# A graph layer on one core: Sel's transfers on another queue, sign counts spread over tiles, products in larger groups, and the residual added after the loop

## The chip, the cores and the metric

The kernel runs on one core of one Trainium2 chip. The metric is the device time of one execution in microseconds (us), lower is better. The core has five engines with a queue of instructions each: PE (TensorE, matrix products), DVE (VectorE), ACT (ScalarE), POOL (GpSimd) and SP (SyncE, which here only issues DMAs). DMAs can be issued from SP, ACT and POOL. Each queue is worked in order, so an instruction that waits holds up all that is behind it.

## The reference

The graph has 6,250 nodes with 128 channels, and 206,250 edges sorted by their destination (100,000 random pairs in both directions, and a loop at each node). W is 128 x 256, b has 128 elements.

```python
h = maximum(layernorm(x), 0)
feat = concatenate([h[dst], h[src] - h[dst]], axis=-1)
msg = feat @ W.T + b
out = segment_max(msg, dst, num_segments=6250)
return x + where(isfinite(out), out, 0)
```

A message splits into a part of the destination and a part of the source: with A = h (W1 - W2)^T + b and B = h W2^T, where W1 and W2 are the halves of W, the message of an edge is A[dst] + B[src]. A[dst] is the same for all edges of a node, so the output is x + A + the maximum of B over the node's sources.

## The kernel before

**Layout.** The nodes are cut two ways. By destination: partition p of 128 holds 49 nodes (LD = 49), and loads from the edge lists a window of 1,792 edges (WIN) that begins at its first one. By source: 6,250 = 50 x 125, a source is row q (0 to 49) and place l (0 to 124). A one-hot product over l can fetch B of one source for each node from the table Bp, which holds B in SBUF. What this dense path can't take, the repeated hits of a node in one row q, is left to a stream of up to 512 residual edges per partition (NS = REST = 512), gathered from DRAM.

**Prologue (0 to 191 us of the profile).**
- x is loaded in seven groups of eight rows q (`load_x`, line 290), 0 to 2 on SP and ACT, 3 to 6 on SP behind a small DVE memset each. `moments` (lines 360, 362) and `scales` (368, 372, 373) give the mean and the deviation.
- `step` makes two rows q of A and B: normalise and transpose (`norm`, `turn`, 549, 554), `relu` (558), `weigh` (564, 566), `keep_all` (ACT's copy to a tile `ba`, 571), `piece` and `less` (574, 578). There are two `ba` tiles, each of two steps, so a copy into one waits for the landing of the `store` from it (586), which SP issues. 27 calls of `step` are written into the program by hand: six ahead of the tests, the others between other work.
- DVE finds the windows: the number of blocks below (343), a gather of one block (98), a count in it (401), then gathers of dwin (destinations) and swin (sources). Lines 616 to 624 make the keys.
- 46 tests, each a DVE comparison of the keys with themselves shifted (493; 501 and 507 for the last three), which PE adds up into `dup` by an identity matrix (488), find repeated pairs. The last two tests compare with the bounds LOb and HIb. There are three tiles `eq` between DVE and PE.
- Eleven moves and `spread` pack the residual edges: `ridx` their sources, `sdl` their destinations.
- POOL writes constants meanwhile: Sel (440), LOb and HIb (458, 459, 28 memsets), and others. Sel, the selector of a row q, goes through DRAM (SelD): it is written, patched in four places and read back (466 to 472), on SP.

**Main loop (191 to 905 us).** 13 tiles of ten partitions' nodes (490 columns; the last tile has 392), each 25 pairs of rows i, i+1: 325 pairs, numbered k. In a pair:
- `some(mats, ...)`: PE makes a few of the 140 small products (246) of the next tile's V, whose factors are the one-hot tiles OHQ (ACT's signs, 203) and OHD (DVE, 208). Once all are done, four steps follow, one a pair: copy out (251), `diff` (255), `rows_u` (258), `rows_t` (261, 262). They end in Vf, which holds for each node and row q the place l.
- `z_and_onehot` of the next pair: PE's z (738), ACT's oh (739).
- PE's four products ps with Bp (786), and DVE's maximum with acc2 (788 for the first pair of a tile, then 790).
- the stream: `gather_group` issues eight gathers of B rows from DRAM on POOL (98) into one of six tiles G; `stream_step` takes one row per partition (163), a running maximum within a node, and SP stores each finished group to M (167). `RATE` says how many rows are due after pair k: int(1.65 (k + 1)).
- ACT's signs and DVE's values for the tile after the next.

Two things stand beside this. In tile 1, `sign(c)` counts for each of 49 + 1 limits how many residual edges are below it (748, 50 in all, two a pair); at the start of tile 3 DVE makes from these the row of M that holds each node's result (`last_e`). In the last tile, A is loaded to `xa` (770), x in four pieces to `xo` (807), and DVE adds them (812) between the pairs.

**End (905 to 951 us).** When the stream is through, POOL issues 49 gathers from M (`extract`, 98). For each group of eight, PE transposes the accumulator, DVE takes the maximum with the gathered rows (850), adds xa (855), and SP and ACT store the output (862).

The counts that the change touches most stand in these lines:

```python
def sign(c):
    dump = two.tile([P, NS], BF16, name="dump", bufs=1)
    A_.activation(dump, sdl, AF.Sign, scale=2.0, bias=nbias[:, c:c + 1], accum_out=ends[:, c:c + 1])
...
while state["ran"] < min(NS, int((k + 1) * RATE)):
    if state["gathered"] < NG and state["ran"] >= (state["gathered"] - GB + 1) * U:
        gather_group()
    stream_step()
```

Of the kernel before, what the change touches and what calls it, by code (L numbers as in the profile page):

```python
# [29 lines left out]
F32 = mybir.dt.float32  # L30
BF16 = mybir.dt.bfloat16
# [9 lines left out]
P = 128  # L41
# [6 lines left out]
L = 125  # L48
LD = 49
# [3 lines left out]
U = 8  # L53
# [9 lines left out]
def gnn_kernel(tc, x, src, dst, W, b, out):  # L63
    nc = tc.nc
# [36 lines left out]
    with ExitStack() as ctx:  # L101
# [10 lines left out]
        with ExitStack() as body:  # L112
# [154 lines left out]
            with ExitStack() as pre:  # L267
# [79 lines left out]
                blk = swin[:, :SB]  # L347
                gather(blk, dst.rearrange("(b s) -> b s", s=SB), below_i[:, 0:1])

                kk = pool.tile([P, REST], F32, name="kk")  # L350
# [59 lines left out]

                for g in (3, 4, 5, 6):
                    xg[g] = rows.tile([P, U, C], F32, name="G") if g < 6 else pool.tile([P, Q % U, C], F32, name="xt")
                    V.memset(xg[g][:L, 0, 0:1], 0.0)
                    load_x(g, (nc.sync, nc.sync))

                for i in range(2):
# [20 lines left out]

                LOb = work.tile([P, W2], BF16, name="LOb", bufs=1)
                HIb = work.tile([P, W2], BF16, name="HIb", bufs=1)
                G_.memset(Sel.rearrange("p q m -> p (q m)").bitcast(F32), 0.0)  # L440
# [13 lines left out]
                for j, f in enumerate((100.0, -100.0)):  # L454
                    G_.affine_select(out=adj[:, j:j + 1], in_=adj[:, j:j + 1], compare_op=ALU.not_equal, fill=f,
                                     base=1 - P, pattern=[[0, 1]], channel_multiplier=1)
                for b in range(NBLK):
                    G_.memset(LOb[:, b * P:(b + 1) * P], float(lo[b] + 1))
                    G_.memset(HIb[:, b * P:(b + 1) * P], float(hi[b] + 1))
                G_.iota(nbias, pattern=[[-2, LD + 1]], base=-1, channel_multiplier=0,  # L460
# [4 lines left out]

                nc.sync.dma_start(SelD, Sel)
                for i, k in enumerate((0, 64)):
                    nc.sync.dma_start(at(SelD, k * Q * (L + 1), [[(Q + 1) * (L + 1), Q], [1, L + 1]]), dg[:, i])
                for q in range(2):
                    nc.sync.dma_start(SelD[Q + q:Q + q + 1], cm[Q + q:Q + q + 1].rearrange("p (o m) -> p o m", o=1)  # L470
                                      .to_broadcast([1, Q, L + 1]))
                nc.sync.dma_start(Sel, SelD)

# [140 lines left out]
                for _ in range(6):  # L614
                    step()
                V.tensor_scalar(dlf, dwin, thr, 1.0, op0=ALU.subtract, op1=ALU.add)
                V.tensor_scalar(dlc, dlf, 0.0, float(LD + 1), op0=ALU.max, op1=ALU.min)
# [12 lines left out]
                for n, f in enumerate(tests):  # L630
                    f()
                    if n % 8 == 5:
                        step()
                    elif n % 5 == 2 and early:
                        turned(*early.pop(0))
                    if n in (16, 32):
                        moments(3 + n // 32)
                        scales_a(3 + n // 32)
                    if n in (18, 34):
                        scales_b(3 + n // 32)  # L640
# [79 lines left out]
            with ExitStack() as main:  # L720
# [21 lines left out]
                def some(fs, left):  # L742
                    for f in fs[:-(-len(fs) // max(left, 1))]:
                        fs.pop(0)()

                def sign(c):
                    dump = two.tile([P, NS], BF16, name="dump", bufs=1)
                    A_.activation(dump, sdl, AF.Sign, scale=2.0, bias=nbias[:, c:c + 1], accum_out=ends[:, c:c + 1])  # L748

                oh = z_and_onehot(*pairs[0])  # L750
                soon, hot_fs = list(onehots(1)), [[], []]
                mats, rest = [], []
                RATE = 1.65
                XG = 13
# [3 lines left out]
                for k, (t, i) in enumerate(pairs):  # L758
# [18 lines left out]

                    if t or not (soon[0] or soon[1]):
                        some(mats, left - 4)
                    nxt = z_and_onehot(*pairs[k + 1]) if k + 1 < len(pairs) else None  # L780
# [8 lines left out]
                    else:  # L789
                        V.tensor_tensor(acc2[:, :, :n], acc2[:, :, :n], ps[:, :, :n], ALU.max)  # L790
                    while state["ran"] < min(NS, int((k + 1) * RATE)):
                        if state["gathered"] < NG and state["ran"] >= (state["gathered"] - GB + 1) * U:
                            gather_group()
                        stream_step()
                    if state["ran"] == NS and not Rt:
                        for d in range(LD):
                            extract(d)
                    if xa is not None and i >= 16 and (i - 16) % 8 == 0 and (i - 16) // 8 * XG < LD:

                        d0 = (i - 16) // 8 * XG  # L800
                        d1 = min(d0 + XG, LD)
                        xo = fin.tile([P, XG, C], F32, name="xo", bufs=2)
                        if d1 > LASTD:
                            V.memset(xo[96:], 0.0)
                        for p0, p1, g in ((0, P - 16, d1), (P - 16, P - 1, d1), (P - 1, P, min(d1, LASTD))):
                            if g > d0:
                                nc.sync.dma_start(xo[p0:p1, :g - d0],
                                                  at(x, (p0 * LD + d0) * C, [[LD * C, p1 - p0], [1, (g - d0) * C]]))
                        adds.append((d0, d1, xo))
                    if adds and (i - 16) % 8 == 6:  # L810
                        d0, d1, xo = adds.pop(0)
                        V.tensor_add(xa[:, d0:d1], xa[:, d0:d1], xo[:, :d1 - d0])  # L812
                    for fs in soon:
                        some(fs, 10 - i // 2)
                    for fs in hot_fs:
                        some(fs, left)
                    oh = nxt
                    if i == Q - 2:
# [3 lines left out]
                                          for j in range(2)), ALU.max)  # L822
                    if t == 1:
                        sign(i)
                        sign(i + 1)
                    if t == 3 and i == 0:

                        V.tensor_scalar(ends, ends, -0.5, 0.5 * NS, op0=ALU.mult, op1=ALU.add)
                        V.tensor_tensor(has, ends[:, 1:], ends[:, :LD], ALU.is_gt)
                        V.tensor_scalar(ends, ends, -1.0, 0.0, op0=ALU.add, op1=ALU.max)  # L830
                        V.tensor_scalar(ends, ends, rowbase, float(-P * NS), op0=ALU.add, op1=ALU.add)
                        V.tensor_tensor(has, has, ends[:, 1:], ALU.mult)
                        V.tensor_scalar_add(last_e, has, float(P * NS))
# [6 lines left out]
                T_.matmul(p[:1, 0, :16], ones[:, :1], badc, start=True, stop=True)  # L840
                acc_v = acc.rearrange("c (p d) -> c d p", d=LD)
                for d0 in range(0, LD, U):
                    g = min(U, LD - d0)
                    o = fin.tile([P, U, C], F32, name="o", bufs=2)
                    for j0 in range(0, g, 4):
# [79 lines left out]
```

## Time and profile before

| | us |
|---|---|
| median of three runs | 954.12 |
| lowest and highest | 952.63, 956.5 |
| the profiled execution | 952.84 |
| its span | 951.0 |
| PE busy | 773.3 (81%) |
| DVE busy | 763.7 (80%) |
| ACT busy | 654.1 (69%) |
| POOL busy | 561.1 (59%) |

The span runs from the first to the last instruction of the program in one profiled execution; its own device time is 1.84 us longer. A busy time is the union of an engine's instructions. Times in timelines count from the start of the span, L12 is line 12 of the kernel, and what stands in brackets behind an instruction is how long its engine was idle before it and what ended that. PEld is PE's loading of weights. PEclk is the share of full clock that PE was granted. A tile's name on the left of an arrow is what is written, on the right what is read.

### The profile page before, as it was taken

The page shows a single profiled execution, that of the slowest core. Times are in us where ns is not written, and L with a number is a line of the kernel's source. Part 1 is how long each engine was busy: PE and PEld are TensorE (multiplying, and loading weights), DVE is VectorE, ACT ScalarE, POOL GpSimd, SP SyncE. Part 2 cuts the span into 40 slices and gives each one's busy share as a digit, 9 for nine tenths or more (in the row PEclk, how much of TensorE's full clock was granted, in tenths as well). Part 3 has the DMA queues.
Part 4 walks back from the last instruction along what each step waited for, and adds up shares of the span by engine and source line. Part 5 has one row for each costly group of instructions (what it writes and reads, how often), then busy time and mean ns, then how long its engine had stood idle before and what let it go on. Part 6 is the DMA issues. An engine that isn't in the chain of part 4 may idle for free.

```text
span 951.0 us, 14067 instructions
## 1 busy us (share of the span) xinstructions
PE 773.3 (81%) x4277; PEld 535.0 (56%) x4277; DVE 763.7 (80%) x1799; ACT 654.1 (69%) x1623; POOL 561.1 (59%) x632
## 2 busy tenths in 40 slices
PE   1949658879887789898989898999989898976540
PEld 0424335446555467676767676676767676755430
DVE  5739999785766669897989899798979899996742
ACT  1403484796799988887888888798978887554200
POOL 3300000077777767777777777777777777731774
PEclk9969955685778779997999899899979999998865
DMA  5531011223223223333333333333333333337442
GB/s 139 155 105 44 22 42 46 76 73 97 90 81 97 76 92 119 96 105 111 95 98 119 95 121 97 96 119 97 118 96 109 109 100 114 114 105 229 111 135 82
DMA packets 50518, 95.73 MB, mean 101 GB/s; under 512 B 12209, under 2 KB 31318, under 8 KB 50081
## 3 DMA queue, kind: packets, MB, share of 16 engines
q1 hardware_dynamic: 31108, 55.39, 17.3%
q0 software_dynamic: 18320, 38.92, 15.7%
q10 hardware_dynamic: 1009, 0.49, 0.3%
q8 instruction: 34, 0.56, 0.2%
q14 instruction: 47, 0.39, 0.1%
HBM read 50.05 MB, written 44.64 MB: 100 GB/s over the span
## 4 chain that ended last, share of the span: by engine, by line
PE 57%; ACT 20%; POOL 6%; DVE 6%; DMA 6%; issue 4%; SPq 1%; POOLq 0%; ACTq 0%; DVEq 0%
PE ps L786 25%; PE z L738 16%; PE pv L246 10%; ACT oh L739 7%; ACT OHQ L203 5%; POOL G L98 4%; ACT dump L748 4%; PE pm L564 2%; DVE eq L493 1%; DMA At<-ba 1%; DMA xo<-in_x 1%; DMA SelD<-Sel 1%; PE pv L255 1%; PE dup L488 1%; ACT Vf L262 1%
## 5 line engine op out<-in xcount | busy, mean ns | idle before, releaser
L98 POOL DMA_INDIRECT G<-Bt,ridx x512 | 492.7, 962 | 236.9 <-issue 135.2
L786 PE MATMUL ps<-oh,Bp 126*128 126x490 f32 (+1 forms) x1300 | 435.6, 462 | 20.2 <-DVE acc L790 16.1
L790 DVE TENSOR_TENSOR acc<-acc,ps 128x980 f32<-128x980 f32 (+1 forms) x312 | 360.8, 1157 | 84.7 <-PE ps L786 83.5
L739 ACT ACTIVATE oh<-z 126x490 fp32r<-126x490 f32 (+1 forms) x650 | 336.1, 570 | 134.8 <-PE z L738 134.2
L786 PEld LDWEIGHTS ps<-oh,Bp 126*128 126x128 f32 x1300 | 272.0, 211 | 102.0 <-DVE acc L790 23.8
L738 PE MATMUL z<-Vf,Sel 114*126 114x490 f16 (+1 forms) x650 | 222.0, 421 | 43.9 <-ACT Vf L262 26.8
L203 ACT ACTIVATE OHQ<-TQ,sbias 128x140 bf16<-128x140 bf16 (+1 forms) x637 | 221.3, 408 | 0.6
L163 DVE SCALAR_TENSOR_TENSOR G<-G,slim 128x128 f32<-128x128 f32 x511 | 179.1, 350 | 9.1 <-DMA G<-Bt,ridx 2.0
L246 PEld LDWEIGHTS <-OHQ 128*51 128x51 bf16 x1792 | 108.4, 180 | 101.8 <-issue 91.1
L246 PE MATMUL pv<-OHD,OHQ 128*51 128x13 bf16 (+5 forms) x1638 | 123.4, 244 | 7.7 <-ACT OHQ L203 7.7
L738 PEld LDWEIGHTS <-Sel 114*126 114x126 f16 x650 | 74.0, 146 | 43.2 <-issue 30.5
L208 DVE SCALAR_TENSOR_TENSOR OHD<-TD,TV 128x30 bf16<-128x30 bf16 (+5 forms) x637 | 87.8, 185 | 0.0
L98 POOL DMA_INDIRECT G<-M,last_e x48 | 50.6, 1053 | 46.7 <-DVE xa L812 32.3
L564 PE MATMUL pm<-wT,hT 128*125 128x256 f32 x100 | 48.0, 580 | 20.6 <-ACT hT L558 20.6
L200 POOL MEMSET OHQ<- 128x140 bf16 x4 | 0.8, 227 | 80.8 <-DMA At<-ba 80.8
L488 PE MATMUL dup<-eq,identb 128*128 128x512 bf16 (+1 forms) x184 | 41.5, 366 | 5.0 <-DVE eq L493 2.4
L564 PEld LDWEIGHTS pm<-wT,hT 128*125 128x125 f32 x100 | 22.8, 278 | 28.0 <-ACT hT L558 27.0
L493 DVE TENSOR_TENSOR eq<-KA 128x1792 bf16<-128x1792 int16 x21 | 22.8, 1085 | 18.8 <-PE dup L488 18.8
L748 ACT ACTIVATE dump<-sdl,nbias 128x512 bf16<-128x512 f32 x50 | 35.9, 718 | 0.8
L574 ACT CAST Bp<-pm 125x256 fp32r<-125x256 f32 x50 | 18.5, 370 | 21.0 <-PE pm L578 20.1
L488 PEld LDWEIGHTS <-identb 128*128 128x128 bf16 x184 | 18.4, 101 | 24.1 <-issue 9.5
L788 DVE COPY acc<-ps 128x980 f32<-128x980 f32 (+1 forms) x13 | 15.1, 1163 | 14.9 <-PE ps L786 14.7
(196 smaller groups left out, 420.9 us busy)
## 6 DMA issues: line engine op xcount, KB each, us to landing
M<-G SPq DMA_DIRECT2D x64, 512.0 KB
G<-Bt,ridx POOLq DMA_INDIRECT x512
xa<-At SPq DMA_DIRECT2D x1, 2744.0 KB
G<-in_x SPq DMA_DIRECT2D x6, 448.0 KB
Bt<-ba SPq DMA_DIRECT2D x12, 224.0 KB
At<-ba SPq DMA_DIRECT2D x12, 224.0 KB
xo<-in_x SPq DMA_DIRECT2D x3, 728.0 KB
out_x<-o SPq DMA_DIRECT2D x3, 512.0 KB
```

Source lines behind the costliest of these rows:

```text
L98: G_.indirect_dma_start(out=o, out_offset=None, in_=table, in_offset=bass.IndirectOffsetOnAxis(ap=idx, axis=0))
L163: V.scalar_tensor_tensor(G[:, j], state["prev"], slim[:, k:k + 1], G[:, j], op0=ALU.min, op1=ALU.max)
L203: A_.activation(oq[:, a, :, :nl], TQ[:, :, ls], AF.Sign, scale=2.0, bias=sbias[:, a:a + 1])
L208: V.scalar_tensor_tensor(o[:, bs_, :nl], TD[:, bs_, ls], float(d + 1), TV[:, bs_, ls], op0=ALU.is_equal, op1=ALU.mult)
L246: T_.matmul(o, oq[:, :, b_, l], r, start=k == 0 and b_ == 0, stop=b_ == NBLK - 1, skip_group_check=True)
L488: T_.matmul(dup[:, c0:c1], identb, e[:, c0:c1], start=s == 1, stop=s == SH + 3)
L564: T_.matmul(pm[:L, j], st["hT", i][:, j, :L], wT, start=j == 0, stop=False, skip_group_check=True)
L738: T_.matmul(z[:, :n], Sel[:, i + j], Vf[t % 2][:, :n], start=True, stop=True)
L739: A_.activation(oh[:, j, :n], z[:, :n], AF.Relu)
L748: A_.activation(dump, sdl, AF.Sign, scale=2.0, bias=nbias[:, c:c + 1], accum_out=ends[:, c:c + 1])
L786: T_.matmul(ps[:, j, :n], Bp[:, e, i + j], oh[:, j, :n], start=e == 0, stop=e == 1)
L790: V.tensor_tensor(acc2[:, :, :n], acc2[:, :, :n], ps[:, :, :n], ALU.max)
```

## The change

- Sel's six DMAs are issued on POOL's queue instead of SP's.
- x's groups 4, 5 and 6 are loaded later: 4 after the six steps that precede the tests, 5 and 6 after tests 4 and 8. Their DVE memsets go.
- The 28 memsets of LOb and HIb stand right after the gather of the block.
- `sign(c)` runs once every four pairs, from pair 48 to pair 244 (so one in tile 1, and 49 in tiles 2 to 9); `last_e` is made at pair 248.
- V's products are made in every second pair only, twice as many each time (14, then 13; the last six in pair 20).
- The signs of OHQ are spread over the first 20 pairs of a tile instead of 25.
- The stream is due at 2.05 rows a pair in tile 0 and 1.6 after it.
- xo's first two pieces are loaded in pairs 8 and 16 of the last tile and added after the loop, the other two loaded and added after it.

```diff
                 gather(blk, dst.rearrange("(b s) -> b s", s=SB), below_i[:, 0:1])
+                LOb = work.tile([P, W2], BF16, name="LOb", bufs=1)
+                HIb = work.tile([P, W2], BF16, name="HIb", bufs=1)
+                for b in range(NBLK):
+                    G_.memset(LOb[:, b * P:(b + 1) * P], float(lo[b] + 1))
+                    G_.memset(HIb[:, b * P:(b + 1) * P], float(hi[b] + 1))
...
-                for g in (3, 4, 5, 6):
-                    xg[g] = rows.tile([P, U, C], F32, name="G") if g < 6 else pool.tile([P, Q % U, C], F32, name="xt")
-                    V.memset(xg[g][:L, 0, 0:1], 0.0)
-                    load_x(g, (nc.sync, nc.sync))
+                xg[3] = rows.tile([P, U, C], F32, name="G")
+                V.memset(xg[3][:L, 0, 0:1], 0.0)
+                load_x(3, (nc.sync, nc.sync))
...
-                for b in range(NBLK):
-                    G_.memset(LOb[:, b * P:(b + 1) * P], float(lo[b] + 1))
-                    G_.memset(HIb[:, b * P:(b + 1) * P], float(hi[b] + 1))
...
-                nc.sync.dma_start(SelD, Sel)
+                G_.dma_start(SelD, Sel)
                 for i, k in enumerate((0, 64)):
-                    nc.sync.dma_start(at(SelD, k * Q * (L + 1), [[(Q + 1) * (L + 1), Q], [1, L + 1]]), dg[:, i])
+                    G_.dma_start(at(SelD, k * Q * (L + 1), [[(Q + 1) * (L + 1), Q], [1, L + 1]]), dg[:, i])
                 for q in range(2):
-                    nc.sync.dma_start(SelD[Q + q:Q + q + 1], cm[Q + q:Q + q + 1].rearrange("p (o m) -> p o m", o=1)
+                    G_.dma_start(SelD[Q + q:Q + q + 1], cm[Q + q:Q + q + 1].rearrange("p (o m) -> p o m", o=1)
                                       .to_broadcast([1, Q, L + 1]))
-                nc.sync.dma_start(Sel, SelD)
+                G_.dma_start(Sel, SelD)
...
                 for _ in range(6):
                     step()
+                load_x(4, (nc.sync, nc.sync))
...
                     f()
+                    if n in (4, 8):
+                        load_x(5 + n // 8, (nc.sync, nc.sync))
...
+                def load_xo():
+                    d0 = (adds[-1][1] if adds else 0)
+                    d1 = min(d0 + XG, LD)
+                    xo = fin.tile([P, XG, C], F32, name="xo", bufs=2)
+                    if d1 > LASTD:
+                        V.memset(xo[96:], 0.0)
+                    for p0, p1, g in ((0, P - 16, d1), (P - 16, P - 1, d1), (P - 1, P, min(d1, LASTD))):
+                        if g > d0:
+                            nc.sync.dma_start(xo[p0:p1, :g - d0],
+                                              at(x, (p0 * LD + d0) * C, [[LD * C, p1 - p0], [1, (g - d0) * C]]))
+                    adds.append((d0, d1, xo))
+
+                def add_xo(n):
+                    d0, d1, xo = adds[n]
+                    V.tensor_add(xa[:, d0:d1], xa[:, d0:d1], xo[:, :d1 - d0])
...
-                RATE = 1.65
+                def due(k):
+                    return min(NS, int(2.05 * min(k, NP_) + 1.6 * max(k - NP_, 0)))
...
-                    if t or not (soon[0] or soon[1]):
-                        some(mats, left - 4)
+                    if (t or not (soon[0] or soon[1])) and i // 2 % 2 == 0:
+                        some(mats, (left - 4) / 2)
...
-                    while state["ran"] < min(NS, int((k + 1) * RATE)):
+                    while state["ran"] < due(k + 1):
...
-                    if xa is not None and i >= 16 and (i - 16) % 8 == 0 and (i - 16) // 8 * XG < LD:
...
-                    if adds and (i - 16) % 8 == 6:
-                        d0, d1, xo = adds.pop(0)
-                        V.tensor_add(xa[:, d0:d1], xa[:, d0:d1], xo[:, :d1 - d0])
+                    if xa is not None and i in (16, 32):
+                        load_xo()
...
-                    for fs in hot_fs:
-                        some(fs, left)
+                    for fs, late in zip(hot_fs, (5, 0)):
+                        some(fs, left - late)
...
-                    if t == 1:
-                        sign(i)
-                        sign(i + 1)
-                    if t == 3 and i == 0:
+                    if k % 4 == 0 and 0 <= k // 4 - NP_ // 2 <= LD:
+                        sign(k // 4 - NP_ // 2)
+                    if k // 4 - NP_ // 2 == LD + 1 and k % 4 == 0:
...
+                for n in range(2):
+                    add_xo(n)
+                    load_xo()
                 for d0 in range(0, LD, U):
                     g = min(U, LD - d0)
+                    if d0 + g > adds[1][1] >= d0:
+                        add_xo(2)
+                        add_xo(3)
```

More of the change, by code (lines that the diff above doesn't have):

```diff
@@ L435, in gnn_kernel @@
                     scales_b(g)
-                LOb = work.tile([P, W2], BF16, name="LOb", bufs=1)
-                HIb = work.tile([P, W2], BF16, name="HIb", bufs=1)
                 G_.memset(Sel.rearrange("p q m -> p (q m)").bitcast(F32), 0.0)
@@ L742, in some @@
                 def some(fs, left):
-                    for f in fs[:-(-len(fs) // max(left, 1))]:
+                    for f in fs[:math.ceil(len(fs) / max(left, 1))]:
                         fs.pop(0)()
@@ L797, in gnn_kernel @@
                             extract(d)
-                    if xa is not None and i >= 16 and (i - 16) % 8 == 0 and (i - 16) // 8 * XG < LD:
[L800 to L809, printed above, removed]
-                    if adds and (i - 16) % 8 == 6:
-                        d0, d1, xo = adds.pop(0)
-                        V.tensor_add(xa[:, d0:d1], xa[:, d0:d1], xo[:, :d1 - d0])
+                    if xa is not None and i in (16, 32):
+                        load_xo()
                     for fs in soon:
                         some(fs, 10 - i // 2)
-                    for fs in hot_fs:
-                        some(fs, left)
+                    for fs, late in zip(hot_fs, (5, 0)):
+                        some(fs, left - late)
                     oh = nxt
```

## The prediction

> **What bounds the kernel now.** I read the busy time by tile first. A tile is one of the 13 rounds of the main loop (25 pairs of rows i, i+1), cut at the DVE copy of line 788 that opens each. One tile and the two ends stand out.
>
> ```profile
> core 0: us, PE busy (x) PEld busy (x) DVE busy (x) ACT busy (x) POOL busy (x), PEclk, DMA share, GB/s
> 191.10:262.85 71.75, 60.23 (x303) 41.89 (x303) 51.13 (x165) 57.25 (x155) 54.52 (x60) 0.71 0.30 90
> 262.85:342.16 79.31, 60.51 (x296) 40.20 (x298) 47.12 (x117) 78.19 (x204) 60.12 (x64) 0.78 0.29 85
> 342.16:392.52 50.36, 47.97 (x296) 34.68 (x298) 45.79 (x117) 43.06 (x104) 36.24 (x39) 0.95 0.33 102
> ...
> 442.73:495.01 52.28, 49.89 (x296) 35.66 (x298) 45.87 (x116) 42.96 (x104) 38.61 (x42) 0.90 0.33 101
> 495.01:545.04 50.03, 47.14 (x296) 34.05 (x298) 45.83 (x116) 43.18 (x105) 38.14 (x40) 0.97 0.34 106
> ```
>
> Tiles 2 to 11 take 50.85 us on average ((850.63 - 342.16) / 10), with PE, DVE and ACT all close to full. Tile 1 takes 79.31, with ACT busy for 78.19 of it. The same cut for line 748 alone shows why: the 50 sign counts (each with a read of its sum) all sit there, 0.8 us each.
>
> ```profile
> 262.85:342.16 79.31, 40.00 (x100) 0.78 0.29 85
> ```
>
> Ahead of the tiles I read the waits of 14 to 110 us, then the timeline of SP's queue. The first shows the tests of DVE waiting 15.4 us for PE, which waits 13 us for ACT's copy to ba, which waits for the landing of a store. The second shows why the store is late: it is queued behind Sel's four groups of transfers, each waiting for the one ahead.
>
> ```profile
> DVE eq L493 <- PE dup L488: 19.2, 6, 15.4
> ...
> ACT ba L571 <- DMA At<-ba: 14.0, 1, 14.0
> PE pm L578 <- ACT ba L571: 13.0, 1, 13.0
> ```
> ```profile
> 33.10 0.26 SPq L466 DMA_DIRECT2D SelD<-Sel  x1
> 43.91 0.65 SPq L468 DMA_DIRECT2D SelD<-dg  x2
> 44.61 1.50 SPq L470 DMA_DIRECT2D SelD<-cm  x2
> 47.78 0.27 SPq L472 DMA_DIRECT2D Sel<-SelD  x1
> 48.16 0.83 SPq L586 DMA_DIRECT2D Bt<-ba  x2
> 49.03 5.57 SPq L586 DMA_DIRECT2D At<-ba  x2
> ```
>
> The end is POOL's: 49 gathers from M in a row, and 76.0 us from the first (874.97) to the end of the span. The last gather from Bt was long done (841.69), and DVE's last stream step ran at 865.7. Between them stand SP's queue and DVE's wait for xo (timelines of POOL, DVE and SP):
>
> ```profile
> 841.69 0.94 POOL L98 DMA_INDIRECT G<-Bt,ridx  x1 [0.31 <-issue]
> 874.97 0.94 POOL L98 DMA_INDIRECT G<-M,last_e  x1 [32.34 <-DVE xa L812]
> ```
> ```profile
> 872.94 1.89 DVE L812 TENSOR_TENSOR xa<-xa,xo 128x1664 f32<-128x1664 f32 x1 [6.05 <-DMA xo<-in_x]
> ```
> ```profile
> 859.60 1.16 SPq L807 DMA_DIRECT2D xo<-in_x  x3
> 866.03 0.35 SPq L167 DMA_DIRECT2D M<-G  x1
> ```
>
> The gathers don't need xa; they need the last M store, issued at 866.03 behind 728 KB of xo and 2.7 MB of At on the same queue. I read the named DVE as standing for that store.
>
> **The change part by part**, against the profiled execution: span 951.0, its time 952.84 (1.84 around it), 1.28 under the median of 954.12.
>
> *Sel's six DMAs to POOL's queue.* On SP the stores no longer stand behind them: the first can go when ba is full (ACT's second copy, 32.6) and must land by about 47. Its slowest landing in the trace is 11.4 us, beside a Sel transfer; 32.6 + 11.4 = 44. So PE's 13.05 us (48.55 to 61.60) go, and about 1.5 us more: that idle stretch put PE at half clock until 67.6, over some 5 us of work that took twice its time. Between 0 (another transfer as late) and 14.5 I take 14.5. On POOL the six precede the OHQ memset (112.22) and the Bt gathers (190.24). The chain took 33.1 to about 61 on SP; even twice that ends by 90. If that cover were gone, each us would move the gathers.
>
> *x's groups 4 to 6 later.* Six SP issues of about 1.5 us each move behind stores; group 4 is first read at 93 us, groups 5 and 6 after 120. They leave 20 to 33 us, where DVE waited 4.03 for dwin. That gains nothing, as PE is in its six steps until 42.5 and the tests wait for it. Cost 0.
>
> *LOb and HIb's 28 memsets forward.* 28 x 0.14 = 3.9 us move from 26.4 into POOL's idle stretch after the block gather (10.46 to 18.0). But DVE's chain of one-source fp32 operations runs there (lines 380 to 391, from 10.86), and feeds begin_i, dwin and the six steps. The nearest row, in DVE's timeline, is line 616, beside the same memsets:
>
> ```profile
> 27.26 4.10 DVE L616 TENSOR_SCALAR dwin<-dwin,thr 128x1792 f32<-128x1792 int32 x1 [4.03 <-DMA dwin<-in_dst,begin_i]
> ```
>
> Its neighbours of that size take 1.09, and it ended when POOL's run ended (31.4): 3.0 us lost. The Trainium skill (SBUF — State Buffer, "Who interferes with whom") says that such a DVE operation and a GpSimd one exclude each other, the later waiting for one instruction. By that rule each of about six DVE operations loses up to 0.14, 0.8 us together; by the row, DVE waits for the whole run, 14.4 - 10.86 = 3.5. I take the row: +3.5, range 0 to 3.6. The prologue sums to -11, the Bt gathers starting at 179.
>
> *Ends counted in tiles 2 to 9.* 50 x 0.8 = 40 us leave tile 1. At ACT's 38 us of other work it becomes a tile like the rest: 79.3 to 51, -28.3. Tiles 2 to 9 get 5.0 each: 43.0 + 5.0 = 48.0 of ACT in 51. The signs of OHQ are also drawn into 20 pairs: 3 in each of pairs 0 to 8, then 2. With oh at 0.93 a pair, a sign 0.35 and a count 0.2 on average, ACT needs 2.19 in pairs 0 to 8, 1.84 in 9 to 19.
>
> *Groups of 14.* A PE pair with 7 products takes 1.915 (z at 451.48, 453.39), one without 1.31 (485.42, 486.73). Seven cost 0.60, of which 7 x 0.045 are theirs and 0.29 the change to and fro. Eleven groups in place of 20 save 2.6 a tile: PE 1.31 x 25 + 6.3 + 3.2 + 1.1 = 43.4 a tile at full clock. The products end one pair later (pair 20), so Vf is ready only in pair 23; freed of signs, ACT reaches it sooner. PE waited 2.08 there:
>
> ```profile
> 490.27 0.57 PE L738 MATMUL z<-Vf,Sel 114*126 114x490 f16 x2 [2.08 <-ACT Vf L262]
> ```
>
> I take about 1.2. A tile from 2 to 9 is then 9 x 2.19 + 11 x 1.84 + about 9.4 for the last five pairs = 49.3, and 1.5 for stretches at half clock: 51 for 50.85. Over 10 tiles +1.5.
>
> *Stream paced by tile.* 40 rows a tile in place of 41.25. A gather takes 1.25 (0.94 and 0.30 between):
>
> ```profile
> L98 POOL DMA_INDIRECT G<-Bt,ridx x512 | 492.7, 962 | 236.9 <-issue 135.2
> ```
>
> So POOL needs 50.0 a tile, just inside 51, and 640 in all. Tile 0 takes 51 rows; POOL makes 57 in its 71.75. The last row moves from pair 310 to 312: at 1.39 a pair in tile 12, +2.8.
>
> *x added at the end.* xo's first load is issued while At's is running out, its second after the last M store, and no add stands in DVE's queue. From the last stream step to the first extraction: 9.0 to about 3.5 (an M store alone), -5.5. Four adds (1.9) and two memsets (1.45), 10.5 us, move behind the loop, where DVE waited 4 to 5 us for each four gathers: 0. If that cover were gone, they would all count.
>
> Sum: -11 - 28.3 + 1.5 + 2.8 - 5.5 = -40.5; 951.0 - 40.5 = 910.5, and 1.84: **912**.
>
> **The rivals.**
> *POOL sets the end.* With tiles at 49 or less the loop runs into the gathers: 179 + 640 + 6 to the first extraction, + 76 = 901, time 903; if DVE loses nothing to the memsets, 900. For: tile 1 is 50 us of POOL. Chance 0.17.
> *ACT lags in tiles 2 to 9.* If the 2.19 of pairs 0 to 8 adds to the half-clock stretch that opens a tile, a tile is 53: +20, 932. For: ACT at 48 of 51. Against: POOL and DVE keep leads. 0.14.
> *The store is late again.* SelD<-Sel now runs beside the first stores. If a wait of 11 us remains: 923. 0.10.
> *Slower: PE falls to half clock through tiles 2 to 9.* A count holds oh back by 0.8 every fourth pair, PE idles, and the clock drops as in tile 1 (0.78), where a pair took 3.08. Half a clock costs 1 - 1.915 / 3.08 = 0.38 of the time it lasts. The gain of 40.5 over 8 tiles is 5.1 a tile, that is 13.3 us more at half clock: it decides at a granted clock of 0.81. At 0.75 it costs 7.4 a tile, 59 in all, 971. The Trainium skill (TensorE: Matmul & The Clock Gate, Part 1) has the clock drop only after an idle window of some 3.4 us, which would mean none here. The trace is harsher: a gap of 2.08 at a tile's end goes with 0.90 in the row of 442.73. By the rule a tile would be 49.3 and the sum 897; I keep the row's dips. Against the rival: PE had work for about two thirds of tile 1, and will have it for six sevenths of these (43.4 of 51). 0.05.
> *Nothing happens* would need both the counts and the store to be covered; tile 1's row excludes it. 0.02.
>
> **How the numbers follow.** The forecast itself has 0.52 (904 to 920). Range 897 to 934: it holds the first four cases and the bounds of the memsets (0 to 3.6) and the store. No change is within 0.5%, about what a measurement of this kernel can tell. Faster 0.93, same 0.02, slower 0.05.
>
> **What would show it.** Right: no wait of PE for ba; tile 1 near 51 with counts in tiles 1 to 9, 5.0 us of ACT each; granted clock 0.90 or more in tiles 2 to 9; gathers from Bt with no idle beyond 0.3; no line 812 wait ahead of the first extraction, about 835. DVE's line 380 long, with begin_i 3.5 us later, shows the memsets' price. Wrong: tiles over 53, clock under 0.85, or Bt gathers that start after 185.

## The result, and the profile after

The kernel after takes 921.99 us (median of 4 runs, 919.82 to 923.55) against 954.14 for the kernel before: a ratio of 0.9659, 95% interval 0.9631 to 0.9688, that is 32 us less. The profiled execution took 919.82, with a span of 918.0. The last four experiments below ran on another chip, where the kernel before took 1271.45 and every kernel shows a granted clock of about 0.74 to 0.76; their times stand beside that one only.

The busy time by tile, cut where the first accumulator copy of a tile starts (columns: stretch and length, then busy time and instructions of each engine, granted clock, DMA share, GB/s):

```profile
core 0: us, PE busy (x) PEld busy (x) DVE busy (x) ACT busy (x) POOL busy (x), PEclk, DMA share, GB/s
179.60:247.00 67.40, 52.39 (x309) 37.32 (x308) 54.11 (x175) 56.46 (x155) 51.31 (x56) 0.88 0.32 99
247.00:296.90 49.90, 46.32 (x299) 33.26 (x298) 44.97 (x115) 42.47 (x107) 37.79 (x40) 1.00 0.35 106
296.90:349.30 52.40, 46.12 (x291) 33.03 (x291) 45.08 (x117) 45.62 (x117) 39.84 (x42) 0.94 0.33 102
349.30:398.20 48.90, 45.75 (x304) 33.89 (x302) 45.28 (x116) 46.26 (x119) 37.08 (x39) 1.00 0.35 107
...
806.00:852.00 46.00, 32.09 (x142) 26.25 (x143) 31.52 (x48) 18.61 (x42) 23.82 (x26) 0.81 0.65 177
```

Tile 1 is a tile like the others (79.31 before), at full clock (0.78 before). Tiles 2 to 11 take 50.91 on average ((806.0 - 296.9) / 10), against 50.85, although they now hold 49 of the 50 counts. These rows look like the forecast, except the last: from the start of tile 12 to the first gather from M it takes 35.4 us, and took 24.3 (850.63 to 874.97).

POOL's timeline gives the four moments that the rest is told by (start, length, instruction, idle time before it and what ended that):

```profile
179.09 1.04 POOL L98 DMA_INDIRECT G<-Bt,ridx  x1 [77.79 <-ACT oh L740]
...
830.81 0.94 POOL L98 DMA_INDIRECT G<-Bt,ridx  x1 [0.30 <-issue]
841.39 0.94 POOL L98 DMA_INDIRECT G<-M,last_e  x1 [9.63 <-DVE acc L812]
```

In the kernel before, the first gather from Bt and the start of tile 12 stand here (the others are in the prediction):

```profile
190.24 0.97 POOL L98 DMA_INDIRECT G<-Bt,ridx  x1 [77.64 <-ACT oh L739]
...
850.63 0.97 DVE L788 COPY acc<-ps 128x784 f32<-128x784 f32 x1
```

| us | before | after | difference |
|---|---|---|---|
| start to first gather from Bt | 190.24 | 179.09 | -11.15 |
| first to last gather from Bt | 651.45 | 651.72 | +0.27 |
| last gather from Bt to first from M | 33.28 | 10.58 | -22.70 |
| first gather from M to the end | 76.03 | 76.61 | +0.58 |
| span | 951.0 | 918.0 | -33.0 |

So the whole gain lies in two places: the gathers begin 11 us earlier, and the loop, which used to end 33 us behind POOL's last gather, now ends 10.6 behind it. The gathers themselves take as long as ever. DVE's waits show the turn. Before (engine, line, what it waited for, us in total, times, longest):

```profile
DVE G L163 <- DMA G<-Bt,ridx: 2.0, 2, 1.7
```

and after:

```profile
DVE G L163 <- DMA G<-Bt,ridx: 58.0, 81, 2.7
```

Before, rows lay ready nearly always when the stream step came for them. Now the step comes for rows that have not landed, 81 times. POOL is idle only the 0.3 us between two gathers nearly everywhere: the queue of gathers has become what sets the pace.

### The profile page after: what moved, and what is told of

Read it like the earlier page. It is cut to its first block, busy times and chain, and to the rows that moved or that the text cites. A ratio compares the mean times of both kernels' runs of the same rounds, so it can differ in the third digit from the quotient of the medians.

```text
span 918.0 us, 14090 instructions
## 1 busy us (share of the span) xinstructions
PE 730.2 (80%) x4277; PEld 506.8 (55%) x4277; DVE 757.7 (83%) x1796; ACT 637.0 (69%) x1623; POOL 563.3 (61%) x638
## 4 chain that ended last, share of the span: by engine, by line
DMA 24%; POOL 18%; DVE 18%; PE 16%; issue 13%; ACT 9%; POOLq 0%; ACTq 0%; DVEq 0%
DMA G<-Bt,ridx 23%; POOL G L98 18%; DVE acc L812 6%; PE ps L808 4%; ACT oh L740 3%; PE pm L562 3%; DVE G L163 3%; ACT OHQ L203 3%; DVE OHD L208 2%; PE z L739 2%; DVE eq L491 2%; PE dup L486 2%; PE pt L552 1%; PE pv L246 1%; DVE acc L810 1%
## 5 line engine op out<-in xcount | busy, mean ns | idle before, releaser
L808 PE MATMUL ps<-oh,Bp 126*128 126x490 f32 (+1 forms) x1300 | 406.3, 436 | 45.7 <-DVE acc L812 35.4
L740 ACT ACTIVATE oh<-z 126x490 fp32r<-126x490 f32 (+1 forms) x650 | 339.9, 584 | 115.5 <-PE z L739 114.3
L808 PEld LDWEIGHTS ps<-oh,Bp 126*128 126x128 f32 x1300 | 249.9, 200 | 140.2 <-DVE acc L812 76.1
L739 PE MATMUL z<-Vf,Sel 114*126 114x490 f16 (+1 forms) x650 | 207.6, 395 | 24.5 <-ACT Vf L262 16.6
L246 PEld LDWEIGHTS <-OHQ 128*51 128x51 bf16 x1792 | 96.4, 184 | 51.0 <-issue 50.7
L739 PEld LDWEIGHTS <-Sel 114*126 114x126 f16 x650 | 81.7, 141 | 45.3 <-issue 22.1
L246 PE MATMUL pv<-OHD,OHQ 128*51 128x13 bf16 (+5 forms) x1638 | 100.8, 241 | 4.7 <-DVE OHD L208 3.1
L562 PE MATMUL pm<-wT,hT 128*125 128x256 f32 x100 | 46.5, 564 | 21.4 <-ACT hT L556 21.4
L863 PE MATMUL pf<-ident,acc 128*128 128x128 f32 x49 | 12.6, 423 | 34.0 <-DVE o L864 32.2
L864 DVE TENSOR_TENSOR o<-G,pf 128x512 f32<-128x512 f32 x12 | 8.2, 686 | 33.3 <-DMA G<-M,last_e 33.3
```

The costliest lines, as they stand in the source:

```text
L246: T_.matmul(o, oq[:, :, b_, l], r, start=k == 0 and b_ == 0, stop=b_ == NBLK - 1, skip_group_check=True)
L562: T_.matmul(pm[:L, j], st["hT", i][:, j, :L], wT, start=j == 0, stop=False, skip_group_check=True)
L739: T_.matmul(z[:, :n], Sel[:, i + j], Vf[t % 2][:, :n], start=True, stop=True)
L740: A_.activation(oh[:, j, :n], z[:, :n], AF.Relu)
L808: T_.matmul(ps[:, j, :n], Bp[:, e, i + j], oh[:, j, :n], start=e == 0, stop=e == 1)
```

## The experiments

Theory 1: POOL's 512 gathers from Bt, 651.7 / 511 = 1.275 us apiece from 179 on, set the end, and an edit of the loop counts only as far as it brings the loop down to that pace. Rival: the forecast's sum, in which the loop's edits add up and each is lost when it is undone. "After" is the kernel after, and every edit is made on it unless said otherwise. The kernel before took 953.95 beside experiments 1 to 4 and 954.76 beside 5 to 8, so that their times can be held against 921.99; ratios are to the kernel before.

**1. The loads of the last tile, moved.** The load of xa and the first two pieces of xo go behind the issue of the 49 gathers from M.

```diff
-    nc.sync.dma_start(xa[p0:p1, :g], at(At, ...))   # start of tile 12
...
-    if xa is not None and i in (16, 32):
-        load_xo()
...
     if state["ran"] == NS and not Rt:
         for d in range(LD):
             extract(d)
+        (the load of xa, then load_xo() twice)
```

> The changed kernel with A's load to xa (2.7 MB) and xo's first two pieces moved behind the last M store and the extraction's issue; nothing left out. Theory 1 (gathers from Bt set the pace of the whole loop, the stream runs 3 to 4 rows behind their issue, and xa's load at the start of the last tile holds up gathers in flight): the 7.5 and 5.8 us between DVE's maxima in pairs 3 and 4 of the last tile fall to about 1.5 each, and the last row's landing (6.3) to about 2.5. 922 becomes 908 (904 to 914). Rival (the load only has to take place somewhere: it then holds up the 49 gathers from M instead): the first extraction comes 10 to 14 us earlier, the tail of 76.6 grows by as much, 922 stays.

Measured: 915.64 (ratio 0.9592, 0.9575 to 0.961). In the kernel after, DVE stands in pairs 3 and 4 of tile 12 for rows that POOL had issued in time; SP had just issued the load of At:

```profile
806.13 1.11 SPq L792 DMA_DIRECT2D xa<-At  x3
```
```profile
811.28 0.96 DVE L812 TENSOR_TENSOR acc<-acc,ps 128x784 f32<-128x784 f32 x1
818.56 0.35 DVE L163 SCALAR_TENSOR_TENSOR G<-G,slim 128x128 f32<-128x128 f32 x1 [6.31 <-issue]
...
821.28 0.35 DVE L163 SCALAR_TENSOR_TENSOR G<-G,slim 128x128 f32<-128x128 f32 x1 [1.50 <-DMA G<-Bt,ridx]
824.35 0.35 DVE L163 SCALAR_TENSOR_TENSOR G<-G,slim 128x128 f32<-128x128 f32 x1 [2.72 <-DMA G<-Bt,ridx]
```

The profile names no cause for the 6.31; moving the load is the test of it. POOL stands, too: 2.78, 1.30 and 2.06 us of idle time before its gathers at 819.20, 821.45 and 824.51, the first ended by DVE's stream step, the others by the landing of a gather. With the load moved, POOL goes through tile 12 without a gap (POOL's timeline of the experiment):

```profile
826.20 0.94 POOL L98 DMA_INDIRECT G<-Bt,ridx  x1 [0.30 <-issue]
827.45 0.95 POOL L98 DMA_INDIRECT G<-Bt,ridx  x1 [0.30 <-issue]
828.70 0.94 POOL L98 DMA_INDIRECT G<-Bt,ridx  x1 [0.30 <-issue]
835.34 0.94 POOL L98 DMA_INDIRECT G<-M,last_e  x1 [5.71 <-DVE acc L810]
```

The first gather from M comes 6.05 earlier, although this run reached tile 12 later (810.00 against 806.00). From the start of tile 12 it takes 25.3 in place of 35.4, which is 10.0 less. About 3.8 of that is the landing of the last row: from the last gather to the last stream step it took 6.4 (830.81 to 837.19), with xo's first load issued at 829.50, and takes 2.6 (828.70 to 831.30). The run moves the loads of At and of xo together and does not price them singly.

Some 3.4 is given back: the 48 gathers from M take 69.35 (835.34 to 904.69) where they took 65.9 (841.39 to 907.28), now that the moved loads run beside them; the DMA share of that stretch is 0.64 (834 to 905) against 0.41 (840 to 908). So the rival of the expectation holds for a third of the gain, and what is left of the 10.0 fits the 6.3 between the medians (915.64 and 921.99). Theory 1 had nothing for the 3.4; without it the time would be about 912, inside its 904 to 914.

**2. The memsets back.** LOb's and HIb's 28 memsets stand in their old place.

```diff
                 gather(blk, dst.rearrange("(b s) -> b s", s=SB), below_i[:, 0:1])
-                for b in range(NBLK):
-                    G_.memset(LOb[...]); G_.memset(HIb[...])
...
+                for b in range(NBLK):
+                    G_.memset(LOb[...]); G_.memset(HIb[...])
                 G_.iota(nbias, ...)
```

> The changed kernel with the 28 memsets of LOb and HIb back at their old place on POOL. Theory 1: DVE's line 385 (3.52 us beside the memsets) takes 0.23 again, begin_i, the six steps and the first gather from Bt come 3.3 to 3.5 us earlier, and as the gathers set the pace all of it reaches the end: 918.5. Rival (something later absorbs it, such as PE's six steps or the tests): the first gather from Bt stays at 179 and 922 stays.

Measured: 917.89 (0.9616, 0.9592 to 0.9641), 4.1 less than after. The two intervals overlap at their edges, so the traces are needed. DVE's timeline after:

```profile
10.90 0.28 DVE L384 TENSOR_TENSOR rr<-rr 114x126 f32<-114x126 f32 x1
11.22 3.52 DVE L385 TENSOR_SCALAR r<-rr 114x126 f32<-114x126 f32 x1
14.77 0.23 DVE L386 TENSOR_SCALAR r<-r 114x126 f32<-114x126 f32 x1
```

and in the experiment, where the same operation is line 382:

```profile
10.61 0.23 DVE L382 TENSOR_SCALAR r<-rr 114x126 f32<-114x126 f32 x1
```

One operation of 0.23 us lasts as long as the run of memsets beside it, which in the kernel after begins and ends so:

```profile
10.47 0.23 POOL L352 MEMSET LOb<- 128x128 bf16 x1
...
14.43 0.23 POOL L353 MEMSET HIb<- 128x128 bf16 x1
```

The operation just ahead of it, with two operands to read (line 384), kept its 0.28 beside the same memsets. The first gather from Bt comes at 176.19, 2.9 earlier, and the time is the 918.5 that theory 1 expected, within its noise.

**3. Sel's six DMAs back on SP's queue.**

```diff
-                G_.dma_start(SelD, Sel)
+                nc.sync.dma_start(SelD, Sel)
... (and the other five)
```

> The changed kernel with Sel's six transfers back on SP's queue; x's groups stay late. Theory 1: PE's wait for ACT's copy to ba comes back, 10 to 13 us long, the first gather from Bt starts at 190, and all of it reaches the end: 933 to 936. Rival (x's late groups alone cure the late store, since the queue and the DMA engines are freer): the wait is under 3 us and the time 922 to 925.

Measured: 929.96 (0.9754, 0.9735 to 0.9773), 8.0 more than after. SP's timeline shows the stores behind the chain again; in the kernel after the first goes at 36.26:

```profile
26.80 0.26 SPq L464 DMA_DIRECT2D SelD<-Sel  x1
41.77 0.65 SPq L466 DMA_DIRECT2D SelD<-dg  x2
42.47 1.50 SPq L468 DMA_DIRECT2D SelD<-cm  x2
45.51 0.26 SPq L470 DMA_DIRECT2D Sel<-SelD  x1
45.87 0.83 SPq L584 DMA_DIRECT2D Bt<-ba  x2
```

DVE's tests wait 8.72 us for PE at 63.40 (the longest such wait was 15.4 in the kernel before), and the first gather from Bt comes at 187.50, 8.4 later. All of it reaches the end, as theory 1 wants of anything that moves the gathers' start. But it is less than the 11 to 14 us that were expected (933 to 936): with x's groups late, Sel's chain starts at 26.80 on SP, where it started at 33.10 before.

**4. The counts back in tile 1.**

```diff
-                    if k % 4 == 0 and 0 <= k // 4 - NP_ // 2 <= LD:
-                        sign(k // 4 - NP_ // 2)
-                    if k // 4 - NP_ // 2 == LD + 1 and k % 4 == 0:
+                    if t == 1:
+                        sign(i)
+                        sign(i + 1)
+                    if t == 3 and i == 0:
```

> The changed kernel with all 50 counts in tile 1 and the ends made at the start of tile 3, as before. Rival A, the forecast's sum (tiles add up): tile 1 goes from 49.9 to about 79, the others stay at 50.9: 950. Theory 1 (POOL's gathers set the pace): POOL goes on in tile 1 and builds a lead of 20 rows or more, so tiles 2 to 11 are no longer bound to it and come down to what PE, DVE and ACT need without counts, about 49.3, and xa's load meets a stream with a lead: 930 to 938.

Measured: 922.19 (0.9681, 0.9654 to 0.9708), the time of the kernel after. Its tiles show how that can be:

```profile
246.60:323.80 77.20, 57.49 (x275) 39.56 (x276) 46.56 (x116) 76.31 (x199) 58.31 (x63) 0.76 0.30 87
323.80:369.50 45.70, 43.82 (x297) 33.21 (x297) 45.05 (x116) 41.87 (x107) 34.72 (x37) 1.00 0.35 109
369.50:416.30 46.80, 44.28 (x296) 32.28 (x295) 46.02 (x123) 41.65 (x105) 35.62 (x37) 1.00 0.36 109
...
553.40:602.40 49.00, 45.80 (x296) 33.60 (x295) 45.00 (x117) 41.41 (x105) 37.33 (x39) 0.97 0.35 106
602.40:651.60 49.20, 47.21 (x313) 33.30 (x311) 44.88 (x117) 43.30 (x109) 37.31 (x40) 1.00 0.35 106
```

Tile 1 is back at 77.2 and at a clock of 0.76: the counts cost 27.3 there, as forecast. Meanwhile POOL gathered ahead, and the tiles after it, free of counts, run at 45.2 to 46.8 until that lead is used up. Tile 8 starts at 602.4, against 601.3 after. Both theories had expected a loss here; theory 1 had taken 49.3 us for a tile without counts.

**5. The products in groups of 7 again**, in every pair.

```diff
-                    if (t or not (soon[0] or soon[1])) and i // 2 % 2 == 0:
-                        some(mats, (left - 4) / 2)
+                    if t or not (soon[0] or soon[1]):
+                        some(mats, left - 4)
```

> The changed kernel with V's products made in every pair again, seven at a time. Theory 1 (gathers set the pace at 50.1 us a tile of 40 rows; the loop's engines need about 48.5 with counts and 46 without): PE needs 2.6 us more a tile, which uses up most of the room below the gathers; tiles 2 to 9 go to 51 or 52 and 922 becomes 924 to 934. Rival (the gathers cover all of it): tiles stay at 50.7, 922. Rival (the forecast's view, groups worth 2.6 a tile in full): 922 + 28 = 950.

Measured: 922.19 (0.9664, 0.9648 to 0.968): no loss either, as the rival in the expectation has it. The last gather from Bt stands at 832.0, against 830.81.

**6. One gather in eight left out**, its row taken from the neighbour; the count of stream steps stays.

```diff
                     k = i * U + j
+                    if j == U - 1:
+                        continue
                     gather(G[:, j], ...)
```

> The changed kernel with one gather of eight from Bt left out: the eighth row of each group is not gathered, and the stream's step on it reads the seventh row instead, so DVE's work is the same and POOL has 448 gathers (561 us) in place of 512 (641). Theory 1: tiles 2 to 9 fall from 50.7 to 48 to 49.5, tiles 10 and 11 to about 46, DVE's waits for gathers (58 us) go to under 10, and one execution takes about 890 to 900. Rival (PE, DVE and ACT with its counts set 50.7 a tile, and the gathers only happen to match): tiles 2 to 9 stay within 0.5 of 50.7 and the time within 10 us of 920.

Measured: 876.08 in one run, span 874.3, 44 less than the 918.0 of after. Tiles 2 to 9 take 48.5 on average (387.80 / 8):

```profile
290.20:678.00 387.80, 361.42 (x2359) 269.89 (x2359) 363.86 (x927) 364.15 (x934) 294.45 (x307) 0.97 0.35 107
```
```profile
796.50 0.94 POOL L98 DMA_INDIRECT G<-M,last_e  x1 [44.19 <-DVE acc L814]
```

This is theory 1's test, and it holds: the work of PE, DVE and ACT is the same, yet the tiles are shorter. (A gather's issue and its transfer go together here, so the run does not tell which of the two sets the 1.275.) Tiles 2 to 9 are within the expected 48 to 49.5, but the time went further than the expected 890 to 900: the loop is 6.8 ahead when tile 2 starts (290.15 against 296.93), and tile 12 is 12.0 shorter. For POOL is through with Bt at 752, 44.19 us before the line above, and the load of At does no harm: tile 12 starts at 773.1, and 23.4 us later comes the first gather from M, against 35.4 after.

**7. One rate for the stream**, 1.65 rows a pair as in the kernel before.

```diff
-                    return min(NS, int(2.05 * min(k, NP_) + 1.6 * max(k - NP_, 0)))
+                    return min(NS, int(1.65 * k))
```

> The changed kernel with the stream due at 1.65 rows a pair all along, as before. Theory 1: POOL issues as fast as it can in both, so the last gather ends at the same time; the stream only takes fewer rows in tile 0 and runs some 15 rows behind the gathers, then 41.25 a tile use that up. Tiles 1 to 8 are then not bound to the gathers and come down to 48 to 49, the later ones go to 51.7; the end is within 4 us of 922. Rival (pacing is what keeps the loop from waiting): DVE's waits for gathers (58 us) grow and the time goes up by 5 to 15 us.

Measured: 922.46 (0.9655, 0.9638 to 0.9672): the time as expected, but not the way there. Tile 0 is shorter (61.4), and so is tile 1 (46.5), but there the lead ends: tiles 2 to 11 take 52.5 on average, 1.65 x 25 = 41.25 rows at POOL's pace, where tiles of 48 to 49 were expected up to tile 8. The pacing shares out one fixed amount of gathering.

**8. Memsets back and loads moved**, the edits of 1 and 2 together.

> The changed kernel with the memsets at their old place and A's load and xo's first two pieces behind the last M store: the edits of the runs that were 4.1 and 6.4 us faster, together. If the gathers set the pace from the first one on, the two add up, as one moves the first gather and the other what follows the last but a few: 922 - 10.5 = 911 to 912. If they share a cause (both only free the DMA engines or POOL at the end): 915 to 916.

Measured: 911.51 (910.33 to 912.94; ratio 0.9551, 0.9534 to 0.9567), the fastest of all that leave nothing out, and as expected. First gather from Bt at 174.45, last at 822.37, first from M at 829.03: the two gains add, since one moves the gathers' start and the other lies behind their end.

**9 to 12. Parts undone together, and parts alone**, on the chip with the low clock. In 9, the edits of 4 and 5 together:

> The kernel after with two parts undone together that cost nothing undone singly: the 50 counts back in tile 1, and the products in groups of 7 in every pair. Theory 1 (either part alone keeps the tiles at or under the gathers' pace, and the cover is used once): tile 1 takes 77 to 79, tiles 2 to 11 go at their own pace without counts, 50.85 in the kernel before, which is no faster than the gathers' 50.9, so the 21 rows of lead (26 us) from tile 1 are never used up: 922 + 18 to 24 = 940 to 946, with POOL's last gather from Bt at about 845 to 850, held by its buffers and not by its issues. Theory 2 (POOL's gathers cover this too, the tiles run at 48 or less): 922 to 926, last gather at 832.

In 10, the kernel before with the counts spread (the edit of 4 reversed):

> The kernel before with one part of the change alone: the counts spread over tiles 2 to 9. By the prediction's sum this is 954 - 28 = 926. By theory 1 (the gathers, begun at 190.2 and 641 long, then set the end at 190.2 + 641 + 6 to 13 + 3 + 76 + 9 for the late store): 933 to 938, with tile 1 at 50 to 52, tiles 2 to 9 at 51 to 53 and POOL without waits for buffers after tile 4 or so. If the counts only move to tiles that are full already, with no gap to take them: 950 to 954.

In 11, the kernel before with groups of 14 (the edit of 5 reversed):

> The kernel before with one other part alone: the products in groups of 14 in every second pair; the counts stay in tile 1. By the prediction's sum (2.6 us of PE a tile, but nothing from a tile that ACT holds): at most 954 - 10 x 2.6 = 928, and 952 if ACT takes it up. By theory 1: tile 1 stays at 78 to 79, tiles 2 to 9 run at 46 to 47 until the lead is used up, and the gathers set the end as in the kernel above: 933 to 938, within 4 us of it. Rival (groups of 14 bring nothing without the signs drawn forward): 950 to 954.

In 12, the kernel after up to the loop, the kernel before from there:

> The kernel after up to the main loop, the kernel before from there on: the prologue's part of the change alone. First gather from Bt at 179 to 180. Theory 1: the loop of before goes at its own pace, not POOL's, so the whole 11 us reach the end: 942 to 944. Rival (part of it is lost to waits in tiles 0 and 1): 946 to 950. With the 922 of the kernel after, the difference is what all the loop's edits bring together: 20 to 22 by theory 1.

Measured, beside 1271.45 (1249.07 to 1296.22) for the kernel before: 9 takes 1231.78 (ratio 0.9679, 0.9585 to 0.9774), 10 takes 1254.76 (0.9881, 0.9754 to 1.0007), 11 takes 1285.99 (1.0118, 1.0035 to 1.0201), 12 takes 1274.07 (1242.65 to 1283.4). No expectation can be held against these, as another limit rules there. Experiment 10 shows it, in the groups and then in the waits:

```profile
L98 POOL DMA_INDIRECT G<-Bt,ridx x512 | 487.6, 952 | 498.0 <-issue 139.5
```
```profile
ACT oh L739 <- remote: 197.5, 40, 12.0
...
POOL G L98 <- DMA M<-G: 98.7, 18, 13.9
...
POOL G L98 <- DVE OHD L208: 72.1, 14, 16.7
```

The gathers are as quick as ever (952 ns of one, 962 in the kernel before), but POOL is idle for 498.0 us ahead of them, 236.9 there: it waits for buffers that a slower loop frees late. On this chip the loop, not POOL, sets the pace. The low clock is not all of it: PE is busy for 94 us more than in the kernel before (867.6 against 773.3), but the span is 295 longer, and ACT stands 40 times, 197.5 us in all, for something that the profile calls remote (another core, or a queue that it doesn't know). The kernels profiled on the other chips have no such wait. What it is stays open.

One thing can be taken from these runs. The prologue's part holds: first gather from Bt at 180.10 in experiment 12, with the new prologue, and at 189.50 in experiment 10, with the old one. Whether counts and groups must both be undone for a loss, which experiment 9 was to tell at the ordinary clock, stays open, as does where experiment 9's gain of 40 us on this chip comes from. That the prologue alone (experiment 12) shows none says little, as the times of one kernel lie up to 47 us apart there.

## Why the prediction was right, and where it was not

The time lies in the range that was given (897 to 934), but outside the 904 to 920 of the forecast's own sum, and what sets it is the rival "POOL sets the end", to which the prediction gave a chance of 0.17.

*Prologue, -11: the sum right, its terms not.* The first gather was put at 179 and came at 179.09 (178.5 in experiment 4 and 180.1 in experiment 5, which have the same prologue). The stall of PE for ba is gone. The memsets, +3.5, showed as 3.52 on one line; experiment 2 gives 2.9 at the first gather and 4.1 in the time. The row beside the memsets was the better guide than the rule of the Trainium skill (SBUF — State Buffer, "Who interferes with whom"), by which the estimate was 0.8. But the queue, -14.5, is worth only 8.4 at the first gather when it is undone by itself (experiment 3). By the difference (11.15 - 8.4 + 2.9) about 5.6 came from the late loads of x, which the prediction put at 0: ahead of Sel's chain they held it up. No run undoes them alone, so this share is not shown. That the sum came out so close is in part luck.

*Tile 1, -28.3: the size right (-29.4), its place in the sum wrong.* Experiment 4 puts all of it back, and the total does not move. A tile's time counts only while the loop, and not the gathers, is the later of the two. The sum asked for 29.5 between the first gather from Bt and the first from M (-28.3 + 1.5 + 2.8 - 5.5), which leaves 655.2 of the 684.7 before; 662.3 came. With the loads of the last tile moved it is 655.2 (experiment 1) and 654.6 (experiment 8), of which the gathers from Bt alone take 648.6 and 647.9. So the forecast had asked, without knowing it, for about the least that the gathers allow, and by theory 1 a sum with a larger gain would have missed by all that it added.

*Tiles 2 to 11, 51: 50.9, for another reason.* The prediction made 51 from ACT's pairs (49.3) and 1.5 of half clock. The loop itself can do 48.5 (experiment 6); 50.9 is 40 rows at 1.275. The granted clock was 1.00 in five of tiles 2 to 9 and 0.93 or 0.94 in the other three, so the 1.5 taken for dips was too much; the estimate of 49.3 without dips, by the rule of the Trainium skill (TensorE: Matmul & The Clock Gate, Part 1), was nearer to the loop's own pace. In tile 1 of experiment 4, with 50 counts, it was 0.76 as in the kernel before (0.78): counts in a heap go with a low clock, counts spread out do not, although the longest wait of PE in that tile of experiment 4 is 3.3 us and the next 1.9, shorter than the rule's 3.4. That is also why the slower rival (clock under 0.81 in tiles 2 to 9) did not come.

*The end, +2.8 - 5.5: the step that failed.* From the start of tile 12 to the first gather from M the prediction has 2.7 less than before, and it took 11.1 more. Part of the term is right: from the end of the last stream step (837.54) to the first gather from M (841.39) it is 3.9, where 3.5 was forecast and 9.0 measured before. What has no price in it are the loads of At and xo beside the gathers. In the kernel before, the load of At met a stream with rows in hand: the last gather was issued at 841.69, 24 us ahead of the last stream step. Now it meets gathers that are awaited one by one. With the loads moved, tile 12 takes 25.3 (experiment 1) and 25.4 (experiment 8) up to the first gather from M, and 23.4 where no gathers from Bt are left to meet them (experiment 6), so they account for nearly all of the 11.1; 21.6 was forecast (24.3 - 2.7). Tile 0 gave back 4.35 (71.75 to 67.40) that no step had; which edit did that was not looked for, and by experiment 7, where it is 61.4 at no gain, it is not worth anything.

*The adds of x behind the loop, 0: right.* From the first gather from M to the end it is 76.61 against 76.03, and DVE still waits 33.3 us there for gathers.

*The rivals.* "POOL sets the end" is what happened, though the time fell nearer the main forecast: its 903 counted 640 for the gathers, which take 651.7 (they took 651.45 in the kernel before, so the page had the number; 1.25 apiece left out the longer gaps), and 6 behind the last one, which were 10.6 beside the loads. The forecast of 912 is met by its own sum only in experiment 8, and by chance: there the missing 10 us came from elsewhere. ACT is busy for 44 to 47 us of tiles 2 to 9 and does not lag, and the store is not late.

## What to carry to other kernels

When several engines are nearly full, work out for each the time that it needs from its first to its last instruction, and take the largest after the change: cuts on the other engines add up only until they meet it, and each, undone singly, then costs nothing. Before cutting a lead, look for what the lead absorbs: the bulk loads that a lead of 24 us had covered cost some 10 without it. An idle stretch of one engine is a free place for its work only if no other engine's short instructions run there that it can hold up.

## What the runs showed of the hardware

- A DVE operation of 0.23 us with one operand tile took 3.52 beside a run of 28 GpSimd memsets, 0.15 us apart: it waited for the run, not for one memset. One of 0.28 with two operands ran beside them at its usual length.
- The load of At, issued at 806.13, held back small indirect gathers that had been issued in time: DVE stood for 6.31, 1.50 and 2.72 us, and for no more than 1.07 in that tile with the load moved. Loads moved beside the 48 gathers from M made these 3.4 us longer together.
- The same kernel before took 954 us on two chips and 1271 on a third, where the four kernels profiled show a granted clock of 0.735 to 0.76; there the gathers no longer set the pace, and in experiment 10 ACT stood for 197.5 us without a cause inside the core that the profile could name.
